# Where a relational GNN's second layer adds up its weight matrices: eight bases ahead of the first layer's edges, 22 as steps between its edge tiles

## The chip, the cores and the metric

The kernel runs on one core of a Trainium2 chip, in float32 but for a few small bfloat16 tables. The metric is the device time of one launch in microseconds (us). Three runs of the kernel before took 4658.36, 4662.56 and 4666.1 us; the median is 4662.56.

## The reference

Four parts follow one another: a relational graph network (RGCN) of two layers on 10000 nodes with 512 features, a mixture of experts, a second graph network (GINE) of four layers, and a feed-forward block with quantized weights. The change touches the first part alone, which is this, cut from the reference:

```python
def rgcn_gate_layer(x, row, col, edge_type, basis, att, gate_w, root, bias):
    w = jnp.einsum('rb,bio->rio', att, basis)      # 2 relations, 30 bases of 512x512
    x_j = x[col]                                   # 5000 edges
    msgs = []
    for r in range(NUM_RELATIONS):
        gate = jax.nn.sigmoid(x_j @ gate_w[r, :, 0])
        msgs.append(gate[:, None] * x_j @ w[r])
    msg = jnp.where((edge_type == 0)[:, None], msgs[0], msgs[1])
    agg = jax.ops.segment_sum(msg, row, num_segments=x.shape[0])
    return agg + x @ root + bias

h = jax.nn.relu(rgcn_gate_layer(x, row, col, edge_type, basis1, att1, gate_w1, root1, bias1))
out = rgcn_gate_layer(h, row, col, edge_type, basis2, att2, gate_w2, root2, bias2)
```

The first line of the layer is what the change moves: each relation's 512x512 weight matrix is a sum of 30 matrices ("bases"), each times a number. These sums depend on inputs alone, not on the nodes or edges.

## The kernel before

**Sorting.** `sort_edges` (L217) sorts the edges twice, by source (`by_src`, which the two RGCN layers use, 41 tiles of 128 edges, no tile with edges of both relations) and by target (`by_dst`, which the GINE part uses later). Tables of the sort are stored to memory and read again.

**Node pass.** `rgcn_nodes1` (L725) goes over the nodes in 20 blocks of 512: it loads `x_in`, normalizes it (`xn`, stored to `xn_d`), transposes it on PE and multiplies it by `root` (L742). ACT copies the product out of PSUM (L746), POOL adds the bias (L748), and SP stores the tile `o_nodes` to `r1_d` (the store's line is L139, in the helper `rows_to`). The edges' messages are later added into the same `r1_d`.

**Sums of bases.** `relation_weights` (L625) makes both weight matrices of a layer. For each of the 30 bases SP loads 1 MB into the tile `basis` (L630) out of the pool `stream`, which has two buffers (L755), and DVE adds it, times a number, into the two halves of `ws`, 128x2048 elements each (L635 for the first basis, L637 for the others). That is 60 sums on DVE for each layer.

**Placing.** `place_nodes` (L390) is a generator: it works out, for the GINE part, where the nodes' rows go, in 57 short steps of PE and DVE work. Its first step finds the ends of runs (`ends`), ten steps then compare four tiles of keys each (`equal_keys`, L212, output `eq`), six do tables of counts (`keyrep`, `base`, `row_ends`, `end`, `row_b`, `cum`), and the last 40 look up positions (L554, L567), the first of which also makes `wanted`.

**Edges.** `rgcn_edges` (L640) takes the 41 edge tiles through a pipeline written out by hand: in step i of its loop it

- fetches tile i: POOL gathers 128 rows of `xn_d` (layer 1) or `r1_d` (layer 2) into `x` (L614);
- adds up tile i - 5: PE multiplies `x` by the matrix `same` (L689), which sums rows of equal source, and ACT copies the result to `aT` (L693);
- puts tile i - 6: PE multiplies `aT` by the relation's weights (L703), ACT copies to `o` (L708), and POOL adds the rows into `r1_d` by an indirect DMA, the "scatter" (L619);
- makes tile i - 3 ready: DVE takes two products of `x` and the gate's vector (L669, output `prod`), ACT the sigmoid `g` (L674), DVE the choice by relation (L675, `dots`), PE spreads the keys (L680), and DVE makes `same` (L682);
- takes one step of `beside`, the generator that is handed in.

The loop stands under a manual schedule: PE, POOL, ACT and DVE each do its instructions in the order in which the code names them. Everything outside such a loop is put in order by the framework, which may move work of different parts between one another, and also into the loop's gaps. Each engine then works through its own list strictly in order, and so does SP, which issues the loads and stores of the node pass and of the bases: one that waits holds up all behind it.

Layer 1's loop takes a step of `place_nodes` at i = 6, 8, ..., 46 (21 steps), layer 2's at every i. Layer 2's `relation_weights` stands in the code between the two loops. Layer 2's first gather reads what the last scatter of layer 1 has written.

Of the kernel before, what the change touches and what calls it, by code (L numbers as in the profile page):

```python
# [8 lines left out]
F32 = mybir.dt.float32  # L9
# [4 lines left out]
OP = mybir.AluOpType  # L14
# [3 lines left out]
P = 128  # L18
N = 10000
D = 512  # L20
KC = D // P
# [17 lines left out]
RELATIONS = 2  # L39
# [3 lines left out]
CAP = 625  # L43
CT = (CAP + P - 1) // P
LAYERS = 4
FETCHED, READY = 6, 3
LN_EPS = 1e-5
BN_EPS = 1e-5
# [21 lines left out]
def gnn_ffn_kernel(ctx: ExitStack, tc: tile.TileContext, I, out, dram):  # L70
# [70 lines left out]
    def row_broadcast(pool, d, width, name):  # L141

        t = pool.tile([P, width], F32, name=name)
        nc.sync.dma_start(t, bass.AP(tensor=d.tensor, offset=d.offset, ap=[[0, P], [1, width]]))
        return t
# [477 lines left out]


    def relation_weights(basis, att_d, pool, stream, tag):  # L625
        att = row_broadcast(pool, att_d, RELATIONS * BASES, f"att_{tag}")
        ws = pool.tile([P, RELATIONS, KC * D], F32, name=f"w_{tag}")
        for b in range(BASES):
            t = stream.tile([P, KC, D], F32, name="basis")
            nc.sync.dma_start(t, basis[b].rearrange("(k p) o -> p k o", p=P))  # L630
            tf = t.rearrange("p k o -> p (k o)")
            for r in range(RELATIONS):
                c = att[:, r * BASES + b : r * BASES + b + 1]
                if b == 0:
                    nc.vector.tensor_scalar(ws[:, r], tf, c, None, op0=OP.mult)  # L635
                else:
                    nc.vector.scalar_tensor_tensor(ws[:, r], tf, c, ws[:, r], op0=OP.mult, op1=OP.add)  # L637
        return ws

    def rgcn_edges(tag, meta, src_d, relu, ws, gate_d, dst_d, beside, take):  # L640

        with ExitStack() as s:
# [67 lines left out]
            with tc.manual_schedule(engines={E_.PE, E_.Pool, E_.Activation, E_.DVE}):  # L712
                for i in range(RT + FETCHED):
                    if i < RT:
                        fetch(i)
                    if i >= FETCHED - 1 and i - FETCHED + 1 < RT:
                        add_up(i - FETCHED + 1)
                    if i >= FETCHED:
                        put(i - FETCHED)
                    if READY <= i < RT + READY:  # L720
                        make_ready(i - READY)
                    if take(i):
                        next(beside, None)

    def rgcn_nodes1(root, bias, pools):  # L725

# [25 lines left out]

    with ExitStack() as s:
        wpool = s.enter_context(tc.tile_pool(name="w_rel", bufs=1))
        stream = s.enter_context(tc.tile_pool(name="stream", bufs=2))  # L755
        src_meta = s.enter_context(tc.tile_pool(name="src_meta", bufs=1))
        wk = s.enter_context(tc.tile_pool(name="sort", bufs=1))
        place_wk = s.enter_context(tc.tile_pool(name="place_wk", bufs=1))
        ps = s.enter_context(tc.tile_pool(name="sort_ps", bufs=2, space=PSUM))
        with ExitStack() as n:  # L760
            ld = n.enter_context(tc.tile_pool(name="ld1", bufs=2))
            tp = n.enter_context(tc.tile_pool(name="tp1", bufs=2))
            fix = n.enter_context(tc.tile_pool(name="fix1", bufs=1))
            small = n.enter_context(tc.tile_pool(name="small1", bufs=3))
            pt = n.enter_context(tc.tile_pool(name="pt1", bufs=2, space=PSUM))
            po = n.enter_context(tc.tile_pool(name="po1", bufs=3, space=PSUM))
            zero = fix.tile([P, D], F32, name="zero")
            nc.gpsimd.memset(zero, 0.0)
            for d in (r1_d, a2_d, xf_d, x2_d):
                clear_spare(zero, d)  # L770
            root = load_square(fix, I["L0_gnn_root1"], "root")
            bias = row_broadcast(fix, I["L0_gnn_bias1"], D, "bias")
            by_src = sort_edges(
                "s", I["src"], I["dst"], I["edge_type_2"], by_src_d, wk, ps, src_meta, by_relation=True
            )
            by_src = add_targets(by_src, wk, ps, src_meta)
            by_dst = sort_edges(
                "d", I["dst"], I["src"], I["edge_weight1"].rearrange("e o -> (e o)"), by_dst_d, wk, ps,
                meta_pool,
            )  # L780
            rgcn_nodes1(root, bias, (ld, tp, small, pt, po))
            ws = relation_weights(I["L0_gnn_basis1"], I["L0_gnn_att1"], wpool, stream, "1")
        placing = place_nodes(by_dst, place_wk, ps, meta_pool)
        rgcn_edges(
            "1", by_src, xn_d, False, ws, I["L0_gnn_gate_w1"], r1_d, placing,
            lambda i: i >= FETCHED and i % 2 == 0,
        )
        ws = relation_weights(I["L0_gnn_basis2"], I["L0_gnn_att2"], wpool, stream, "2")
        rgcn_edges("2", by_src, r1_d, True, ws, I["L0_gnn_gate_w2"], a2_d, placing, lambda i: True)
        for _ in placing:  # L790
            pass

# [1028 lines left out]
```

## Time and profile before

| what | value |
| --- | --- |
| time, median of three runs | 4662.56 us |
| time of the profiled execution | 4666.98 us |
| its span, first to last instruction | 4665.2 us |
| mean granted clock of TensorE | 0.931 |
| busy: PE, DVE, ACT, POOL | 87%, 60%, 36%, 34% |
| basis sums after the first of each layer (L637) | 116, 315.8 us together |
| first gather of layer 1 | starts at 532.50 us |
| first gather of layer 2 | starts at 845.12 us |

Times in a profile count from the start of the span. The engines are PE (TensorE's matmuls; PEld is its weight loads), DVE (VectorE), ACT (ScalarE), POOL (GpSimd) and SP (SyncE, which here only issues transfers; its own queue is shown as SPq).

A table of windows has a row for each stretch of time: the busy time of each engine in it with the number of instructions, then the share of TensorE's full clock that was granted (PEclk), the busy share of the DMA engines, and GB/s. A row of a timeline has the start, the length, the engine, the line of the code, the operation, output<-input, and in brackets the idle time before it with what ended that idle time. On SPq the length of a group ("x3") is the time from its first issue to the end of its last. A row of the page's costliest groups has the count, the busy time together with the mean of one in nanoseconds, and the idle time before them with what ended most of it.

The releaser in brackets is inferred. Where the one named had long been done, the wait was for something else, often a transfer.

### The profile page before, as it was taken

The page shows a single profiled execution, that of the slowest core. Times are in us where ns is not written, and L with a number is a line of the kernel's source. Part 1 is how long each engine was busy: PE and PEld are TensorE (multiplying, and loading weights), DVE is VectorE, ACT ScalarE, POOL GpSimd, SP SyncE. Part 2 cuts the span into 40 slices and gives each one's busy share as a digit, 9 for nine tenths or more (in the row PEclk, how much of TensorE's full clock was granted, in tenths as well). Part 3 has the DMA queues.
Part 4 walks back from the last instruction along what each step waited for, and adds up shares of the span by engine and source line. Part 5 has one row for each costly group of instructions (what it writes and reads, how often), then busy time and mean ns, then how long its engine had stood idle before and what let it go on. Part 6 is the DMA issues. An engine that isn't in the chain of part 4 may idle for free.

```text
span 4665.2 us, 42798 instructions
## 1 busy us (share of the span) xinstructions
PE 4046.1 (87%) x13624; PEld 2048.0 (44%) x13624; DVE 2820.7 (60%) x5906; ACT 1679.5 (36%) x2992; POOL 1569.0 (34%) x1127
## 2 busy tenths in 40 slices
PE   6799568897999945968887999999999999999997
PEld 3443234443444422434443555545555455544443
DVE  7887865554545465646755546644575455755776
ACT  4334112232333310116423523354233532334775
POOL 3434334441000036865542113311142111422443
PEclk9899789898988866989889999999999999999998
DMA  8677654457555414986411123102231012311332
GB/s 276 228 260 258 216 123 88 86 105 184 192 171 182 146 48 84 162 164 218 153 54 43 73 77 119 42 17 81 85 108 37 27 75 104 90 30 46 110 109 98
DMA packets 293120, 556.20 MB, mean 119 GB/s; under 512 B 41216, under 2 KB 71969, under 8 KB 291871
## 3 DMA queue, kind: packets, MB, share of 16 engines
q1 hardware_dynamic: 219632, 364.67, 23.2%
q0 software_dynamic: 73264, 188.79, 17.8%
q8 instruction: 111, 1.82, 0.2%
q14 instruction: 113, 0.93, 0.1%
HBM read 292.40 MB, written 260.95 MB: 119 GB/s over the span
## 4 chain that ended last, share of the span: by engine, by line
PE 38%; DVE 8%; DMA 4%; ACT 3%; issue 2%; POOL 1%; POOLq 0%; DVEq 0%; ACTq 0%
PE ps_b L1317 15%; PE ps_d L1317 8%; PE ps_o L1593 5%; PE ps_e L1317 4%; PE ps_x L1424 2%; DMA x<-xg_d,gpos 2%; PE ps_x L1248 2%; ACT feat L1413 1%; DMA x_in<-x_d,node_at 1%; DVE stats L1402 1%; DVE x L1234 1%; DVE feat L1252 1%; PE ps_q L1661 1%; DVE feat L1332 1%; DVE t L1340 0%
## 5 line engine op out<-in xcount | busy, mean ns | idle before, releaser
L1317 PE MATMUL ps_b<-feat,w 128*128 128x512 f32 (+1 forms) x1120 | 499.7, 587 | 25.6 <-ACT feat L1413 25.5
L1317 PE MATMUL ps_d<-feat,w_s 128*128 128x512 f32 (+1 forms) x1120 | 503.6, 586 | 4.3 <-issue 3.1
L1325 ACT ACTIVATE feat<-ps_b,cols 128x512 f32<-128x512 f32 (+1 forms) x300 | 203.8, 683 | 568.1 <-PE ps_b L1317 555.4
L1352 POOL TENSOR_TENSOR feat<-feat 128x1024 f32<-128x1024 f32 (+1 forms) x70 | 162.5, 2322 | 623.2 <-DVE feat L1351 598.2
L1365 POOL TENSOR_TENSOR feat<-feat,p 128x1024 f32<-128x1024 f32 (+1 forms) x70 | 176.3, 2519 | 483.0 <-ACT feat L1325 474.2
L637 DVE SCALAR_TENSOR_TENSOR w<-basis,att,w 128x2048 f32<-128x2048 f32 x116 | 315.8, 2731 | 15.6 <-DMA basis<-in_L_gnn_basis 15.6
L742 PE MATMUL ps_o<-root,xT 128*128 128x512 f32 (+1 forms) x632 | 323.6, 625 | 0.0
L1317 PEld LDWEIGHTS ps_b<-feat,w 128*128 128x128 f32 x1120 | 208.4, 191 | 255.5 <-issue 209.4
L703 PE MATMUL ps_o<-w,aT 128*128 x656 | 304.6, 609 | 0.1
L1426 DVE TENSOR_TENSOR x_rows<-ps_x,be 128x512 f32<-128x512 f32 (+1 forms) x237 | 157.4, 685 | 231.0 <-PE ps_x L1424 231.0
L1317 PEld LDWEIGHTS ps_d<-feat,w_s 128*128 128x128 f32 x1120 | 203.3, 192 | 202.2 <-issue 183.0
L918 PE MATMUL ps_n<-root,rT 128*128 128x512 f32 (+1 forms) x632 | 288.6, 613 | 0.0
L1317 PE MATMUL ps_b<-t,w_s 128*128 128x512 f32 (+1 forms) x560 | 259.2, 603 | 21.7 <-ACT feat L1325 21.6
L1317 PE MATMUL ps_e<-feat,w 128*128 128x512 f32 (+1 forms) x560 | 264.9, 614 | 12.9 <-DVE feat L1283 12.9
L614 POOL DMA_INDIRECT x<-xg_d,gpos x160 | 175.0, 1093 | 287.8 <-issue 71.8
L1317 PE MATMUL ps_b<-feat,w_s 128*128 128x512 f32 (+1 forms) x560 | 253.7, 591 | 0.0
L1413 ACT ACTIVATE feat<-feat,bn_sm 128x512 f32<-128x512 f32 (+2 forms) x320 | 236.6, 809 | 3.4 <-DVE bn_sm L1532 3.4
L1234 DVE SCALAR_TENSOR_TENSOR x<-we,srt_d,x 128x512 f32<-128x512 f32 x160 | 139.9, 889 | 156.6 <-DMA x<-xg_d,gpos 149.5
L1402 DVE BATCH_NORM_STATS2 stats<-feat 128x6 f32<-128x512 f32 (+1 forms) x320 | 202.7, 667 | 46.7 <-POOL feat L1365 33.1
L1248 PE MATMUL ps_x<-same,x 128*128 128x128 f32 x1280 | 176.9, 287 | 58.6 <-DVE same L1244 24.1
L1248 PEld LDWEIGHTS ps_x<-same,x 128*128 128x128 f32 x1280 | 167.9, 199 | 126.9 <-issue 42.2
L1237 ACT ACTIVATE x<-x 128x512 f32<-128x512 f32 x160 | 99.3, 628 | 295.2 <-DVE x L1234 179.3
(483 smaller groups left out, 7656.1 us busy)
## 6 DMA issues: line engine op xcount, KB each, us to landing
basis<-in_L_gnn_basis SPq DMA_DIRECT2D x60, 1024.0 KB
xg_d<-x_rows SPq DMA_DIRECT2D x234, 256.0 KB
xg_d<-x_in SPq DMA_DIRECT2D x39, 512.0 KB
x_in<-in_x SPq DMA_DIRECT2D x19, 1024.0 KB
a_d<-x_in SPq DMA_DIRECT2D x19, 1024.0 KB
xn_d<-xn SPq DMA_DIRECT2D x19, 1024.0 KB
r_d<-o_nodes SPq DMA_DIRECT2D x19, 1024.0 KB
r_in<-r_d SPq DMA_DIRECT2D x19, 1024.0 KB
```

What stands on the lines that cost most here:

```text
L637: nc.vector.scalar_tensor_tensor(ws[:, r], tf, c, ws[:, r], op0=OP.mult, op1=OP.add)
L703: nc.tensor.matmul(ps_o, lhsT=aT[:, k, :], rhs=w_all[:, bass.ds(w0 + k * D, D)], start=k == 0, stop=k == KC - 1,)
L742: nc.tensor.matmul(ps_o[:n], lhsT=xT[:, k, a * P : a * P + n], rhs=root[:, k, :], start=k == 0, stop=k == KC - 1,)
L918: nc.tensor.matmul(ps_o[:n_], lhsT=rT[:, k, a * P : a * P + n_], rhs=root[:, k, :], start=k == 0, stop=k == KC - 1,)
L1234: nc.vector.scalar_tensor_tensor(x, we, by_dst["attr"][:, t : t + 1], x, op0=OP.mult, op1=OP.add)
L1248: nc.tensor.matmul(ps_a[:, k, :], lhsT=x[:, k * P : (k + 1) * P], rhs=same, start=True, stop=True)
L1317: nc.tensor.matmul(ps[fo], lhsT=A[a][:, k, fo * P : (fo + 1) * P], rhs=x[:, k, :], start=first and k == 0, stop=k == 1, skip_group_check=True,
L1325: nc.scalar.activation(dst[:, fo, :], ps[fo], func, bias=b, scale=scale)
L1365: nc.gpsimd.tensor_tensor(b22, b22, p5, OP.add)
L1402: nc.vector.bn_stats(stats[:, k, 2 * p + j, :], big[:, k, s0 + j * w : s0 + (j + 1) * w])
L1413: nc.scalar.activation(hb, hb, AF.Relu, bias=sm[:, fo, 3:4], scale=sm[:, fo, 2:3])
L1593: nc.tensor.matmul(ps_o[:n_], lhsT=big[:, kc, t * P : t * P + n_], rhs=W2[kc], start=kc == 0, stop=kc == KC - 1,)
```

## The change

`relation_weights` now returns the weights' tile and a generator that adds one basis (two sums) at each step. All 30 bases of layer 1 are still added before its edges. Of layer 2's bases, eight (`EARLY_BASES`) are added before layer 1's edges, and the other 22 inside layer 1's edge loop, one at each even i from 4 to 46, behind the work that makes a tile ready. The steps of `place_nodes` move to the odd i from 7 to 45, which is 20 instead of 21; the one left over falls to layer 2's loop, which as before takes one at every i. The pool `stream` has three buffers instead of two.

```diff
--- before.py
+++ after.py
@@ -43,6 +43,7 @@
 CAP = 625
 CT = (CAP + P - 1) // P
 LAYERS = 4
+EARLY_BASES = 8
 FETCHED, READY = 6, 3
 LN_EPS = 1e-5
 BN_EPS = 1e-5
@@ -623,21 +624,26 @@
 
 
     def relation_weights(basis, att_d, pool, stream, tag):
+
         att = row_broadcast(pool, att_d, RELATIONS * BASES, f"att_{tag}")
         ws = pool.tile([P, RELATIONS, KC * D], F32, name=f"w_{tag}")
-        for b in range(BASES):
-            t = stream.tile([P, KC, D], F32, name="basis")
-            nc.sync.dma_start(t, basis[b].rearrange("(k p) o -> p k o", p=P))
-            tf = t.rearrange("p k o -> p (k o)")
-            for r in range(RELATIONS):
-                c = att[:, r * BASES + b : r * BASES + b + 1]
-                if b == 0:
-                    nc.vector.tensor_scalar(ws[:, r], tf, c, None, op0=OP.mult)
-                else:
-                    nc.vector.scalar_tensor_tensor(ws[:, r], tf, c, ws[:, r], op0=OP.mult, op1=OP.add)
-        return ws
-
-    def rgcn_edges(tag, meta, src_d, relu, ws, gate_d, dst_d, beside, take):
+
+        def sums():
+            for b in range(BASES):
+                t = stream.tile([P, KC, D], F32, name="basis")
+                nc.sync.dma_start(t, basis[b].rearrange("(k p) o -> p k o", p=P))
+                tf = t.rearrange("p k o -> p (k o)")
+                for r in range(RELATIONS):
+                    c = att[:, r * BASES + b : r * BASES + b + 1]
+                    if b == 0:
+                        nc.vector.tensor_scalar(ws[:, r], tf, c, None, op0=OP.mult)
+                    else:
+                        nc.vector.scalar_tensor_tensor(ws[:, r], tf, c, ws[:, r], op0=OP.mult, op1=OP.add)
+                yield
+
+        return ws, sums()
+
+    def rgcn_edges(tag, meta, src_d, relu, ws, gate_d, dst_d, beside):
 
 
 
@@ -719,8 +725,7 @@
                         put(i - FETCHED)
                     if READY <= i < RT + READY:
                         make_ready(i - READY)
-                    if take(i):
-                        next(beside, None)
+                    beside(i)
 
     def rgcn_nodes1(root, bias, pools):
 
@@ -752,7 +757,7 @@
 
     with ExitStack() as s:
         wpool = s.enter_context(tc.tile_pool(name="w_rel", bufs=1))
-        stream = s.enter_context(tc.tile_pool(name="stream", bufs=2))
+        stream = s.enter_context(tc.tile_pool(name="stream", bufs=3))
         src_meta = s.enter_context(tc.tile_pool(name="src_meta", bufs=1))
         wk = s.enter_context(tc.tile_pool(name="sort", bufs=1))
         place_wk = s.enter_context(tc.tile_pool(name="place_wk", bufs=1))
@@ -779,14 +784,26 @@
                 meta_pool,
             )
             rgcn_nodes1(root, bias, (ld, tp, small, pt, po))
-            ws = relation_weights(I["L0_gnn_basis1"], I["L0_gnn_att1"], wpool, stream, "1")
+            ws1, adding = relation_weights(I["L0_gnn_basis1"], I["L0_gnn_att1"], wpool, stream, "1")
+            for _ in adding:
+                pass
+            ws2, adding = relation_weights(I["L0_gnn_basis2"], I["L0_gnn_att2"], wpool, stream, "2")
+            for _ in range(EARLY_BASES):
+                next(adding)
         placing = place_nodes(by_dst, place_wk, ps, meta_pool)
+
+        def beside_1(i):
+            if i >= 4 and i % 2 == 0:
+                next(adding, None)
+            elif i > FETCHED:
+                next(placing, None)
+
+        rgcn_edges("1", by_src, xn_d, False, ws1, I["L0_gnn_gate_w1"], r1_d, beside_1)
+        for _ in adding:
+            pass
         rgcn_edges(
-            "1", by_src, xn_d, False, ws, I["L0_gnn_gate_w1"], r1_d, placing,
-            lambda i: i >= FETCHED and i % 2 == 0,
+            "2", by_src, r1_d, True, ws2, I["L0_gnn_gate_w2"], a2_d, lambda i: next(placing, None)
         )
-        ws = relation_weights(I["L0_gnn_basis2"], I["L0_gnn_att2"], wpool, stream, "2")
-        rgcn_edges("2", by_src, r1_d, True, ws, I["L0_gnn_gate_w2"], a2_d, placing, lambda i: True)
         for _ in placing:
             pass
```

## The prediction

> **What bounds the stretch now.** The page says that TensorE is busy for 87% of the span, but the change touches only the stretch between the end of the node pass and layer 2's edges. So I read that stretch first by windows, then each queue's timeline.
>
> ```profile
> core 0: us, PE busy (x) PEld busy (x) DVE busy (x) ACT busy (x) POOL busy (x), PEclk, DMA share, GB/s
> 440.00:510.00 70.00, 69.07 (x205) 31.80 (x204) 54.03 (x38) 23.49 (x45) 29.49 (x9) 1.00 0.69 220
> 510.00:541.00 31.00, 0.18 (x1) 0.00 (x0) 20.88 (x11) 0.53 (x1) 11.82 (x8) 0.57 0.78 259
> 541.00:626.00 85.00, 33.84 (x105) 18.92 (x105) 80.00 (x98) 8.49 (x19) 21.23 (x11) 0.68 0.69 199
> 626.00:845.00 219.00, 180.47 (x676) 98.34 (x675) 104.97 (x397) 45.16 (x105) 93.10 (x68) 0.95 0.48 84
> ```
>
> Four stages with four limits. Until 510 the node pass fills PE, and sums of bases on DVE lie beside it for nothing. Until 541 PE is empty. Until 626 DVE is full (80.00 of 85) and PE waits. From 626 neither PE nor DVE is full, though DVE has 114 us idle. I look for the cause of the empty 31 us in the timelines of SP and POOL.
>
> ```profile
> 504.88 12.51 SPq L630 DMA_DIRECT2D basis<-in_L_gnn_basis  x3
> 517.49 0.46 SPq L139 DMA_DIRECT2D r_d<-o_nodes  x1
> ...
> 522.18 1.21 SPq L139 DMA_DIRECT2D r_d<-o_nodes  x2
> ```
>
> ```profile
> 507.14 7.70 POOL L748 TENSOR_TENSOR o_nodes<-o_nodes,bias 128x1024 f32<-128x1024 f32 x2 [4.43 <-ACT o_nodes L746]
> 532.50 3.14 POOL L614 DMA_INDIRECT x<-xn_d,gidx_s  x1 [17.66 <-DVE w L637]
> ...
> 572.38 3.51 POOL L619 DMA_INDIRECT r_d<-o,sidx  x1 [2.32 <-DVE dots L675]
> ...
> 649.32 1.59 POOL L619 DMA_INDIRECT r_d<-o,sidx  x1 [2.55 <-ACT g L674]
> ...
> 834.20 1.55 POOL L619 DMA_INDIRECT r_d<-o,sidx  x1 [3.93 <-issue]
> 839.71 1.55 POOL L619 DMA_INDIRECT r_d<-o,sidx  x1 [3.95 <-DMA r_d<-o,sidx]
> 845.12 1.01 POOL L614 DMA_INDIRECT x<-r_d,gidx_s  x1 [3.86 <-DMA r_d<-o,sidx]
> ```
>
> The last bias add ends at 514.84, but its r1_d store stands on SP behind basis loads that wait for DVE to free one of two buffers, and goes out only at 522.18. The first gather of layer 1 shares memory with these tiles, starts at 532.50, and the first product with the gate starts at 540.99. Scatters of layer 1 form a chain: each waits for the one before to land, 839.71 − 834.20 = 5.5 us apart. Last, DVE in the steady part, first and last line one pair of tiles apart:
>
> ```profile
> 642.83 0.34 DVE L212 SCALAR_TENSOR_TENSOR eq<-ps_s,key_d,below 128x128 f32<-128x128 f32 x1
> ...
> 649.18 0.16 DVE L675 SCALAR_TENSOR_TENSOR dots<-g,of_rel 128x2 f32<-128x2 f32 x1 [3.25 <-ACT g L674]
> ...
> 653.62 0.16 DVE L675 SCALAR_TENSOR_TENSOR dots<-g,of_rel 128x2 f32<-128x2 f32 x1 [2.41 <-ACT g L674]
> ...
> 654.22 0.34 DVE L212 SCALAR_TENSOR_TENSOR eq<-ps_s,key_d,below 128x128 f32<-128x128 f32 x1
> ```
>
> A pair takes 11.39 us, against 11.0 for two scatters: the chain of scatters is nearly the bound, and DVE waits twice for the sigmoid g, which stands on ACT behind the copy of ps_o.
>
> ```profile
> L637 DVE SCALAR_TENSOR_TENSOR w<-basis,att,w 128x2048 f32<-128x2048 f32 x116 | 315.8, 2731 | 15.6 <-DMA basis<-in_L_gnn_basis 15.6
> ```
>
> **The change, part by part.** No instruction is added or removed. What moves, by the written order of both kernels: before, the framework put 24 of layer 2's 60 sums into layer 1's first ten tiles, one behind each DVE instruction, 20 into the second half of the node pass and the rest earlier. After, 16 sums stand before the edges and 44 in the loop, two back to back at even steps. A sum alone is 2.3 us (2.35 in rows of this stretch; the group's mean of 2731 ns takes in ones slowed by transfers).
>
> *Start of the edges.* No basis load waits in front of the last r1_d stores any more, for three are fetched ahead into the three buffers and the next ones come inside the loop. The FFN's small loads now stand before those stores on SP; what they wait for was done by about 490, so I cost them at nothing, and 4 to 7 us if that cover fails. The stores go out at 515 to 516 instead of 522.18. A scatter lands 3.95 us after its issue; before, from the end of the last store's issue to the gather took 532.50 − 523.39 = 9.1 us with basis transfers in flight. I take the near one: gather at 520, bounds 519 to 525. From gather to product took 8.5 us here and 4.25 us at layer 2's start (845.12 to 849.37), where no basis was in flight; as here none will be, I take 4.25. First product at 524.5 instead of 541.0: **16.5 us** earlier (bounds 7 to 19).
>
> *First tiles.* Tiles 0 to 6 take about 2.35 us of DVE each (two products 1.43, sigmoid 0.3, same 0.6): 16.5; three pairs of sums 13.8; place_nodes' step of ends 3.3 (ten small DVE instructions of place_nodes took 733.94 to 736.1, 2.2 us, and this one has two more copies that wait for PE): 33.6 us, where before the same tiles took some 90.
>
> *Ten pairs with a step of equal_keys.* Call its first eq Z. Dots follow at Z + 6.35, as above (649.18 − 642.83). PE's part is unchanged, as PE is released by the second eq. Then same is done at Z + 6.95, two sums to Z + 11.55, the next tile's products 1.43 to 12.98, its sigmoid and same at once, for PE and ACT ran ahead during the sums: next Z at 13.88. So 4.6 us of sums cost **2.5 us**, and the rest goes into the second wait for g. Ten pairs: 138.8 us. The scatters' 11.0 is no longer the bound.
>
> *Seven pairs with place_nodes' later steps* took 733.94 to 815.12 before, 81.2 us; with 2.3 us each 97.3. The last three scatters 16.6 (at 5.5). Sum of the loop 33.6 + 138.8 + 97.3 + 16.6 = 286 against 845.1 − 541.0 = 304.1: 18 us less.
>
> *The clock.* PE would idle about 4.1 us in each of the 17 pairs, while DVE sums. The granted clock fell to half after an idle PE in three places of this stretch, 3.6 to 4.8 us after its last work:
>
> ```profile
> 514.00:515.00 1.00, 0.00 (x0) 0.00 (x0) 1.00 (x1) 0.00 (x0) 0.84 (x1) 0.65 0.02 8
> 515.00:516.00 1.00, 0.00 (x0) 0.00 (x0) 1.00 (x1) 0.00 (x0) 0.00 (x0) 0.50 0.00 0
> ```
>
> PE's last work here ended at 510.18. After a restart at 630.55 it was back at 633.8, so 3.2 us at half speed, a loss of 1.6 us. Bounds per pair 0 and 1.6; 4.1 lies amid 3.6 to 4.8, so I take 0.7, or **12 us** for 17 pairs.
>
> [...]
>
> *Rest.* Two more sums now stand before the last store of the sort: 4.7 us of DVE, of which I count 2, as PE's backlog of transposes and matmuls (69.07 of 70 busy) covers much of it. One place_nodes step moves from layer 1 to layer 2, at most 0.8 us (the median step there has three DVE instructions of 0.48, most of it in DVE's idle time). Layer 2 and the later three stages stay as they are; what is free there starts earlier by the gain.
>
> *The sum.* 16.5 + 18 − 12 − 2 = **20 us**. The profiled execution of before took 4666.98 us (span 4665.2); after: 4647. It lies 4.4 above the median of the three runs, 4662.56, so the median goes to **4643**.
>
> **The rivals.**
>
> *The clock halves in every gap.* 27 instead of 12: gain 5, median 4657, no change that can be told. For it: 4.1 us is longer than the shortest of the three observations. Against it: two of three were longer.
>
> *The chain of scatters stays the bound, and gets slower.* In the early edges of before, with sums and basis transfers beside them, scatters took up to 3.51 us to issue instead of 1.59, and the way from gather to product 8.5 us instead of 4.25. Now each pair has two sums and a load of 1 MB beside it. If each scatter gets 0.5 us longer in issue and 2.1 us in landing, a pair takes 2 × 8.2 = 16.4 us instead of 14.6 (13.88 + 0.7): 17 × 1.9 = 32 us lost, 12 us slower than before, median 4675. This decides from 15.8 us per pair, where 17 × 1.2 eats the 20. For it: chain and DVE are within 3 us of each other. Against it: the window from 510 to 541 moved 259 GB/s, by which a load of 1 MB lasts some 4 us of 14, so it meets one scatter in two at most.
>
> [...]
>
> *More is gained.* The clock holds in every gap: gain 32, median 4631; with a node pass freed of DVE's sums and loads, down to 4620.
>
> *It does not do what it says.* The framework interleaved the sums before as well; if the start at 541 is set by something else than the stores (the trace names a DVE sum as releaser of the first gather), the 16.5 us shrink to 7 and the gain to 10: 4653, about the edge of what can be told.
>
> **How the numbers follow.** Forecast 0.47 (its own range 4627 to 4653), clock at each gap 0.13, slower chain 0.22, more gained 0.10, start that does not move 0.08. The range leaves out the ends of the slow and the large case: 4615 to 4682. A measurement of this kernel tells about 0.2%, 9.3 us, from no change. Faster by over 0.2%: nearly all of the forecast and of the large case, and half of the last, 0.59; within: the clock's case, the rest of the last and edges, 0.19; slower 0.22.
>
> **What would show it.** Right: first gather near 520, r1_d stores on SP without a basis load between them; scatters 14 to 15 us per pair; sums in twos on DVE; the second wait of dots for g gone; layer 2's first gather near 825 and its 232 us unchanged. Wrong: scatters 16 us per pair with each waiting for DMA r_d (slower chain), or a clock below 0.8 in the loop, or a first gather still behind 530.

## The result, and the profile after

The changed kernel took 4664.49 us (median of 12 runs, 4656.93 to 4673.24), the kernel before 4656.73 us in the same job (12 runs, 4646.18 to 4666.10). The ratio is 1.0017, with a 95% interval of 1.0007 to 1.0027: 7.8 us slower, within the 0.2% that I called no change, and on the other side of the forecast 20 us gain. The size rests on this one set of runs: in the four later ones the kernel before had medians of 4662.03 to 4664.37 us, about the time of the changed kernel here. What is sure is that the gain did not come.

The two profiled executions alone would mislead: 4666.98 us before, 4658.06 after, 9 us the other way. In the 17 profiles of this study, what comes behind layer 2's last gather, which no kernel here changes, takes from 3594.8 to 3608.2 us (3608.0 in before's, 3594.8 in after's). So I compare profiles only up to that gather: 1057.17 us before, 1061.54 after, 4.4 us later, of the timing's sign. A second profile of the changed kernel puts it at 1061.41.

Windows of the changed kernel, the same stretches as for before:

```profile
core 0: us, PE busy (x) PEld busy (x) DVE busy (x) ACT busy (x) POOL busy (x), PEclk, DMA share, GB/s
440.00:510.00 70.00, 69.13 (x197) 30.97 (x197) 33.45 (x48) 25.06 (x48) 25.07 (x11) 0.95 0.76 220
510.00:541.00 31.00, 19.39 (x60) 10.01 (x60) 10.73 (x19) 5.87 (x12) 15.04 (x10) 0.78 0.48 159
541.00:626.00 85.00, 64.10 (x213) 35.77 (x211) 57.29 (x140) 15.54 (x36) 35.88 (x22) 0.86 0.57 142
626.00:845.00 219.00, 163.65 (x533) 90.92 (x533) 150.44 (x343) 37.19 (x84) 87.74 (x53) 0.84 0.53 128
```

Of the empty 31 us behind 510, 19.39 are filled with PE work, DVE is no longer full behind 541, and from 626 DVE has 45 us more to do, as intended. But PEclk fell from 0.95 to 0.84 in the long last stretch. The timelines of SP and POOL show the start of the edges:

```profile
512.82 0.35 SPq L145 DMA_DIRECT2D gate<-in_L_gnn_gate_w  x1
515.07 9.74 SPq L140 DMA_DIRECT2D r_d<-o_nodes  x3
541.07 84.73 SPq L634 DMA_DIRECT2D basis<-in_L_gnn_basis  x7
```

```profile
523.22 1.25 POOL L753 TENSOR_TENSOR o_nodes<-o_nodes,bias 16x512 f32<-16x512 f32 x1 [1.13 <-ACT o_nodes L751]
526.93 1.01 POOL L615 DMA_INDIRECT x<-xn_d,gidx_s  x1 [2.46 <-DMA r_d<-o_nodes]
...
604.23 1.59 POOL L620 DMA_INDIRECT r_d<-o,sidx  x1 [6.75 <-ACT g L680]
...
609.62 1.74 POOL L620 DMA_INDIRECT r_d<-o,sidx  x1 [1.73 <-DVE w L641]
...
620.34 1.59 POOL L620 DMA_INDIRECT r_d<-o,sidx  x1 [7.70 <-ACT g L680]
...
852.25 1.01 POOL L615 DMA_INDIRECT x<-r_d,gidx_s  x1 [4.09 <-DMA r_d<-o,sidx]
```

No basis load stands among the r1_d stores, and the first gather follows the last bias add by 2.46 us. But that bias add ends at 524.47 instead of 514.84: the node pass got 9.6 us longer. In the loop a pair takes 620.34 − 604.23 = 16.1 us. POOL waits 6.7 to 8.3 us (4.9 in the first of these pairs), for ACT, ahead of each first scatter of a pair, so the chain of scatters is not the bound. DVE shows one whole pair and more:

```profile
604.09 0.16 DVE L681 SCALAR_TENSOR_TENSOR dots<-g,of_rel 128x2 f32<-128x2 f32 x1 [4.59 <-ACT g L680]
...
604.69 4.60 DVE L641 SCALAR_TENSOR_TENSOR w<-basis,att,w 128x2048 f32<-128x2048 f32 x2
...
610.97 0.16 DVE L681 SCALAR_TENSOR_TENSOR dots<-g,of_rel 128x2 f32<-128x2 f32 x1 [0.33 <-ACT g L680]
...
611.57 0.34 DVE L213 SCALAR_TENSOR_TENSOR eq<-ps_s,key_d,below 128x128 f32<-128x128 f32 x1
...
620.20 0.16 DVE L681 SCALAR_TENSOR_TENSOR dots<-g,of_rel 128x2 f32<-128x2 f32 x1 [5.53 <-ACT g L680]
...
627.69 0.34 DVE L213 SCALAR_TENSOR_TENSOR eq<-ps_s,key_d,below 128x128 f32<-128x128 f32 x1
```

From dots at 604.09 to Z at 611.57 it takes 7.48 us, against 13.88 − 6.35 = 7.53 in the forecast, and the second wait for g is gone. But from Z to the dots it takes 8.63 us instead of 6.35. That part is PE's, and PE and its clock say why (the second fence is a table of windows, same columns as above):

```profile
607.67 0.38 PE L212 MATMUL ps_s<-ident,key_d 128*128 128x128 f32 x2
611.98 0.95 PE L212 MATMUL ps_s<-ident,key_d 128*128 128x128 f32 x2 [3.92 <-DVE eq L213]
612.72 1.92 PE L695 MATMUL ps_a<-same,x 128*128 128x128 f32 x8
```

```profile
606.95:610.36 3.41, 1.10 (x5) 0.38 (x3) 3.38 (x5) 0.58 (x1) 1.68 (x2) 1.00 0.62 138
610.36:613.77 3.41, 1.79 (x7) 1.50 (x8) 2.65 (x14) 0.20 (x1) 1.98 (x2) 0.50 0.86 287
613.77:617.18 3.41, 3.41 (x9) 1.86 (x8) 0.86 (x4) 0.58 (x1) 0.00 (x0) 0.50 0.72 176
617.18:620.60 3.42, 3.42 (x16) 2.00 (x15) 0.29 (x3) 0.80 (x3) 0.26 (x1) 1.00 0.01 2
```

PE ends at 608.05 and waits 3.92 us. The clock is at half from 610.36, before the wait is over, and comes back only at 617.18, 5.2 us after PE has restarted; eight ps_a matmuls take 1.92 us in place of 1.07 (at full clock, at 643.87 in before). The ten pairs with equal_keys run from Z = 563.43 to 723.29, 15.99 us each, and the clock falls once for each, about where it starts. In seven of them it is at half for 6.83 us, and these pairs take 16.1 to 16.7 us; in three for 3.41 us, and these take 15.1 to 15.2.

### The profile page after: what moved, and what is told of

Same layout as the page of the kernel before. It is cut to its first block, busy times and chain, and to the rows that moved or that the text cites. A ratio compares the mean times of both kernels' runs of the same rounds, so it can differ in the third digit from the quotient of the medians.

```text
span 4656.3 us, 42795 instructions
## 1 busy us (share of the span) xinstructions
PE 4061.7 (87%) x13624; PEld 2058.8 (44%) x13624; DVE 2814.8 (60%) x5906; ACT 1681.5 (36%) x2992; POOL 1570.6 (34%) x1127
## 4 chain that ended last, share of the span: by engine, by line
PE 38%; DVE 8%; DMA 4%; ACT 3%; issue 2%; POOL 1%; DVEq 0%; POOLq 0%; ACTq 0%
PE ps_b L1334 14%; PE ps_d L1334 9%; PE ps_o L1610 5%; PE ps_e L1334 4%; PE ps_x L1441 2%; DMA x<-xg_d,gpos 2%; PE ps_x L1265 2%; DVE stats L1419 1%; ACT feat L1430 1%; DVE feat L1269 1%; DMA x_in<-x_d,node_at 1%; DVE x L1251 1%; PE ps_q L1678 1%; DVE feat L1349 1%; DVE t L1357 1%
## 5 line engine op out<-in xcount | busy, mean ns | idle before, releaser
L709 PE MATMUL ps_o<-w,aT 128*128 x656 | 315.2, 626 | 0.0
L641 DVE SCALAR_TENSOR_TENSOR w<-basis,att,w 128x2048 f32<-128x2048 f32 x116 | 301.9, 2619 | 0.0
L1334 PE MATMUL ps_b<-t,w_s 128*128 128x512 f32 (+1 forms) x560 | 250.2, 586 | 17.7 <-ACT feat L1342 17.7
L1368 DVE TENSOR_TENSOR feat<-feat,t 128x1024 f32<-128x1024 f32 (+1 forms) x70 | 83.9, 1198 | 199.4 <-PE ps_b L1334 199.4
```

The costliest lines, as they stand in the source:

```text
L709: nc.tensor.matmul(ps_o, lhsT=aT[:, k, :], rhs=w_all[:, bass.ds(w0 + k * D, D)], start=k == 0, stop=k == KC - 1,)
L1334: nc.tensor.matmul(ps[fo], lhsT=A[a][:, k, fo * P : (fo + 1) * P], rhs=x[:, k, :], start=first and k == 0, stop=k == 1, skip_group_check=True,
```

## The experiments

Theory 1: the granted clock falls in every pair while DVE sums, and that is the loop's loss. Theory 2, the rival of the prediction: the chain of scatters, slowed by sums and loads, sets the pair. The start was open, so one run repeats the kernel.

**after_again**: the changed kernel unchanged.

> The changed kernel once more, for a second profile. In the first one the node pass ended 9.6 us later than before (last bias add ended at 524.47 instead of 514.84) and the key column of the second sort was copied at 483.52 instead of 469.67. If that comes from the order of the sums, it is there again within 3 us. If it is an accident of one execution (the phase of the clock's windows, or transfers), the two times move by more than 3 us. Pairs of edge tiles 15.9 us again by either.

The key column of the second sort was copied at 483.51, the last bias add began at 523.16 and layer 2's first gather at 852.21: each within 0.1 us of the first profile. So the 9.6 us are not an accident of one execution. (The clock's windows are the steps of 3.41 us in which its records change, shown under why the prediction was wrong.) The time was 4664.99 us.

**warm**: extra matmuls at the end of even steps.

```diff
+            def keep_warm():
+                ps_k = pk.tile([P, P], F32, name="ps_k")
+                for _ in range(8):
+                    nc.tensor.matmul(ps_k, lhsT=ident, rhs=ident, start=True, stop=True)
...
                     beside(i)
+                    if not relu and i >= 4 and i % 2 == 0 and i < RT + READY:
+                        keep_warm()
```

> The changed kernel with eight extra matmuls of 128x128 into ps_k at the end of every even step of layer 1's edges, whose result nobody reads; they lie in the 3.9 us in which PE waits for DVE's sums. Theory 1 (the clock): in every pair of tiles PE idles 3.9 us, the granted clock falls to half and costs 2.1 us of a pair's 15.95. With PE busy the clock stays at 1.00, a pair takes 13.9 us, and from the first gather of layer 1 to that of layer 2 it takes 325 - 17 x 2.1 = 290 us; the kernel gets 30 to 35 us faster than the changed one, so about 25 faster than before. Theory 2 (the chain of scatters, slowed by sums and loads, sets 15.95): extra PE work changes nothing or costs up to 1 us per pair, 4664 to 4680.

The kernel took 4674.9 us, ratio 1.0029 (1.0015 to 1.0044): slower. The clock did hold: 1.00 from 545 to 720, and a pair took 14.86 us, 1.1 less than before the extra matmuls, not 2.1. They wait for `same` (PE idle for 1.43 us ahead of them), and so push back the next tile's matmuls, whose result DVE then waited for (1.37 us instead of 0.33). Later steps lost more than the first pairs gained. It told against theory 2, but priced the clock badly.

**warm_late**: the same kind of matmuls behind the odd tile's work, in a place where nothing waits for them.

```diff
             elif i > FETCHED:
+                spare = ps.tile([P, 2 * LO], F32, name="ps_r", bufs=1)
+                for _ in range(10 if i < RT + READY else 0):
+                    nc.tensor.matmul(spare[:, :P], lhsT=ident, rhs=ident, start=True, stop=True)
                 next(placing, None)
```

> The changed kernel with ten extra matmuls of 128x128 in every odd step of layer 1's edges, behind the tile's own work on PE and ahead of place_nodes' step, into a PSUM tile that nothing else uses then (ps_r); nobody reads them. In the run warm the clock held at 1.00, but the extra matmuls stood ahead of the next tile's work, and a pair took 14.9. Here they lie behind it, in the last 3 us of PE's wait. Theory 1 (the clock's fall makes a pair 15.95 instead of 13.88): a pair takes 13.9 us, from first gather to first gather 285 to 300 instead of 325, the kernel 4630 to 4645. If instead the extra time of a pair came from elsewhere and warm's 14.9 was a bound of PE's own work, a pair stays at 14.9 or above and the kernel at 4650 or above.

4644.79 us, ratio 0.9963 (0.9950 to 0.9976). PE and DVE in one pair:

```profile
611.99 2.40 PE L801 MATMUL ps_r<-ident 128*128 128x128 f32 x20
614.23 0.38 PE L212 MATMUL ps_s<-ident,key_d 128*128 128x128 f32 x2
616.31 0.32 PE L212 MATMUL ps_s<-ident,key_d 128*128 128x128 f32 x1 [1.70 <-DVE eq L213]
```

```profile
602.06 0.34 DVE L213 SCALAR_TENSOR_TENSOR eq<-ps_s,key_d,below 128x128 f32<-128x128 f32 x1
...
608.41 0.16 DVE L681 SCALAR_TENSOR_TENSOR dots<-g,of_rel 128x2 f32<-128x2 f32 x1 [3.25 <-ACT g L680]
...
615.90 0.34 DVE L213 SCALAR_TENSOR_TENSOR eq<-ps_s,key_d,below 128x128 f32<-128x128 f32 x1
```

Z to Z is 13.84 us, the forecast's 13.88 without the clock, and dots follow Z by 6.35 again. Work that computes nothing made the kernel 0.5% faster than the changed one, so theory 1 stands for these ten pairs: they took 140.1 us instead of 159.9. In one of them the clock fell all the same, for 3.41 us from 673.44, and this pair (from Z = 671.25 to 686.78) took 15.53 us. The seven pairs with other steps did not gain (105.8 us against 106.1, with a clock of 0.88 from 700 to 835); their excess over the forecast 97.3 is not settled by this. From first gather to first gather it took 310.8, more than expected for that reason.

**in_waits**: one sum in each tile's wait for g, instead of two behind every second tile.

```diff
                 nc.scalar.activation(g[:, :RELATIONS], dots, AF.Sigmoid)
+                inside(t)
...
-            if i >= 4 and i % 2 == 0:
-                next(adding, None)
-            elif i > FETCHED:
+            if i > FETCHED and i % 2 == 1:
                 next(placing, None)
+        def inside_1(t):
+            for _ in range(2 if t < 3 else 1):
+                next(adding, None)
```

> The changed kernel with its 44 sums inside the loop moved: one sum in each tile, between DVE's products and dots, where DVE waits for the sigmoid g (2.4 and 3.2 us in the pairs of the kernel before), two in each of the first three tiles. Theory 1: sums of 2.3 us lie in waits, PE is never idle for more than about 2 us, the clock stays at 1.00, and a pair takes 11.0 (two scatters of 5.5) to 12.5 us; from first gather to first gather 255 to 275 us instead of 325, the kernel 4595 to 4615. Theory 2: sums and loads beside the scatters slow these wherever the sums stand: a pair stays at 14 us or more, 4640 or above.

4637.45 us, ratio 0.9947 (0.9934 to 0.9961): the same 44 sums, at another place in the same list, and 0.7% faster than the changed kernel. DVE between two Z:

```profile
607.31 0.34 DVE L213 SCALAR_TENSOR_TENSOR eq<-ps_s,key_d,below 128x128 f32<-128x128 f32 x1
...
610.33 2.35 DVE L641 SCALAR_TENSOR_TENSOR w<-basis,att,w 128x2048 f32<-128x2048 f32 x1
613.66 0.16 DVE L682 SCALAR_TENSOR_TENSOR dots<-g,of_rel 128x2 f32<-128x2 f32 x1 [0.98 <-ACT g L680]
...
618.70 0.34 DVE L213 SCALAR_TENSOR_TENSOR eq<-ps_s,key_d,below 128x128 f32<-128x128 f32 x1
```

11.39 us, exactly the pair of the kernel before, which has no sums there. But only the three pairs from 595.92 to 630.09 are like this; the other six between the first and the last Z took 13.1 to 13.7. The clock did not stay at 1.00 as expected: it was 0.91 from 545 to 720, and fell at the start of four of the six. And scatters came 12.9 us per pair in this stretch and fell behind, until the loop stopped for them (16.0 us in the pair that ends with the scatter at 637.3). It took 299.7 us from first gather to first gather, not 255 to 275, and the kernel missed the 4595 to 4615 expected. Here theory 2 is half right.

**in_waits_no_loads**: in_waits without the 1 MB loads inside the loop.

```diff
-                t = stream.tile([P, KC, D], F32, name="basis")
-                nc.sync.dma_start(t, basis[b].rearrange("(k p) o -> p k o", p=P))
+                if tag == "1" or b <= EARLY_BASES:
+                    t = stream.tile([P, KC, D], F32, name="basis")
+                    nc.sync.dma_start(t, basis[b].rearrange("(k p) o -> p k o", p=P))
```

> As in_waits, but the 21 last bases of layer 2 are not loaded: their sums take the ninth base again, so the values differ and the 1 MB loads inside the loop are gone. It prices the loads. In in_waits scatters came 12.9 us per pair in the stretch from 560 to 630, where DVE's own pair was 11.4. If the loads in flight slow the scatters' landing, scatters come 11.4 to 11.6 per pair and layer 2's first gather comes 15 to 30 us earlier than 828. If DVE's sums themselves slow them (their issue on POOL), it stays at 12.5 or more.

This kernel leaves out 21 loads and so computes other values. One run of 4609.54 us; layer 2's first gather at 796.20 instead of 828.01, 3 us of it by an earlier first gather of layer 1 (525.26). Scatters on POOL:

```profile
603.20 1.59 POOL L620 DMA_INDIRECT r_d<-o,sidx  x1 [2.73 <-DVE eq L213]
...
608.98 1.59 POOL L620 DMA_INDIRECT r_d<-o,sidx  x1 [2.54 <-ACT g L681]
...
614.51 1.59 POOL L620 DMA_INDIRECT r_d<-o,sidx  x1 [2.65 <-DVE eq L213]
```

11.3 us per pair beside the same sums, from 595 to 630 at a clock of 1.00 as in in_waits: it is the loads in flight that slow the scatters there, by 1.6 us per pair or more, for without them DVE's own pair of 11.39 may set the pace. The sums alone do not make 12.9.

**The number of early bases**, in four kernels. Only the constant (or, in the in_waits kernels, also who gets the remaining sums) differs.

```diff
-EARLY_BASES = 8
+EARLY_BASES = 5      # early_5: 3 bases left for behind the loop
+EARLY_BASES = 18     # early_18: 12 bases left as steps
```

> The changed kernel with 5 instead of 8 of layer 2's bases ahead of layer 1's edges, as many as the kernel before had ahead of the second sort's end; 22 stay as steps and 3 come after layer 1's loop. If sums ahead of the sort's end delayed it, the key column of the second sort is copied 5 us or more earlier than 483.5 and the node pass ends at 520 or before. If the delay is the clock's or an accident, it is as in the changed kernel. The last three bases cost up to 14 us between the layers.

> The changed kernel with 18 instead of 8 of layer 2's bases ahead of layer 1's edges; by the written order the ten more stand behind the second sort's end, where DVE is idle from 483 to 526, and 12 bases are left as steps. Theory 1: the ten fill DVE's idle time while PE ends the node pass; r1_d stores stand behind basis loads again, the first gather comes at 531 to 537 instead of 527; ten pairs lose their sums and go from 15.95 to 11.4 us, so layer 2's first gather comes near 852 + 7 - 45 = 814, the kernel 4620 to 4635. If the node pass itself gets slower by the loads (transfers that its own loads and stores wait for), it ends after 535 and half of the gain is lost.

> As in_waits (one sum in each tile's wait for g), with 5 instead of 8 bases ahead of the edges; the last three bases are added in the first three steps of layer 2's loop, where DVE waits for the last scatters. Theory: sums ahead of the second sort's end delay it. As in early_5, the sort's key column comes 10 us and the first gather 5 us earlier than in in_waits (528.3), and nothing else changes: layer 2's first gather near 823, the kernel 4628 to 4636. If the six sums moved to layer 2 are not hidden, they cost up to 14 us there.

> Both ways together: 18 bases ahead of the edges, and the other 24 sums one by one in the waits for g of every second tile (each of the first eight). In in_waits DVE's own pair was 11.4 us where the clock held, but scatters beside sums and loads came 12.9 us per pair. With half as many sums and loads per pair the scatters come 11.4 to 12 us per pair: from first gather to first gather 265 to 275 instead of 300, the first gather at 531 to 537, the kernel 4612 to 4622. If the chain of scatters is slow for another reason, it stays at 12.9 and the kernel is not below 4635.

early_5 (one run, 4675.2 us): the sort's key column came at 473.69, the first gather at 521.95, 5 us earlier; the three bases behind the loop took it back (layer 2's first gather at 861.33). in_waits_5 (one run, 4648.07): key column 478.80, first gather 527.18, 1.1 us earlier; layer 2's first gather 835.94, 8 us later, and I don't know what took these. early_18, 4667.34 us, ratio 1.0011 (1.0001 to 1.0021): forecast 4620 to 4635, a clear miss. SP and POOL:

```profile
533.82 1.46 SPq L140 DMA_DIRECT2D r_d<-o_nodes  x1
537.88 4.89 SPq L634 DMA_DIRECT2D basis<-in_L_gnn_basis  x2
```

```profile
545.74 1.01 POOL L615 DMA_INDIRECT x<-xn_d,gidx_s  x1 [23.61 <-DMA r_d<-o_nodes]
```

The last r1_d store stood behind basis loads until 533.82 and landed beside two more about 10.5 us after its issue had ended (535.28 to 545.74); the first gather came 18.8 us later than in the changed kernel, and the ten pairs without sums (11.2 to 14 us) gave back only 22. DVE summed without a break until 542, so the idle time it was to fill was shorter than the ten bases. in_waits_18, 4646.95 us, ratio 0.9959 (0.9945 to 0.9973), has the same late start (first gather 555.42) and a loop of 278 us; it missed the 4612 to 4622 expected, too.

**in_waits_11**: 11 bases early, and 38 sums, one in each tile from the fourth.

> As in_waits, with 11 instead of 8 of layer 2's bases ahead of the edges and the other 38 sums one by one in the waits for g of tiles 3 to 40. In early_18 DVE worked on sums until 542 and the stores of r1_d landed beside basis loads 12 us after their issue, so the first gather came at 546. Theory: three more bases end at about 500, well before the node pass (524), so the first gather stays at 525 to 532, the first three tiles lose three sums (7 us), and layer 2's first gather comes near 820 instead of 828; the kernel 4625 to 4635. If any base more ahead of the edges costs what it saves, it is 4637 to 4645.

4639.0 us, ratio 0.9953 (0.9936 to 0.9969). First gather 531.34, layer 2's 817.58, as expected; the time was not below in_waits.

**The third buffer**, taken from the changed kernel and given to the kernel before.

```diff
-        stream = s.enter_context(tc.tile_pool(name="stream", bufs=3))
+        stream = s.enter_context(tc.tile_pool(name="stream", bufs=2))   # bufs_2, bufs_2_timed; before_bufs_3 the other way
```

> The changed kernel with two buffers of bases instead of three, nothing else. The third buffer lets a load go out one base earlier. If it matters to the start, the first gather comes later than 527 by up to one sum pair (5 us) or the second sort's end moves by more than 3 us from 483.5; the pairs of edge tiles stay at 15.9, as their loads have 16 us of time with either.

> The kernel before with three buffers of bases instead of two, nothing else. If the third buffer delays the second sort's end (469.7 before, 483.5 after) by its loads, the key column is copied at 475 or later here; if the order of the sums does, it stays within 3 us of 469.7. The loop's start stays behind basis loads, first gather 530 or later, and the kernel within 10 us of before.

> The changed kernel with two buffers again (as bufs_2), now timed against before. In bufs_2 the second sort ended at 458.4 instead of 483.5 and the first gather came at 503.1 instead of 526.9; layer 2's first gather at 829.4 instead of 852.2. If that is the order that the framework writes for two buffers, it is there again within 1 us, and the kernel takes 4664 - 23 = 4641 (4636 to 4648), 0.3 to 0.6% faster than before. If it was an accident of one execution, the second sort ends near 483 again and the kernel takes 4655 or more.

The copy of the key column on DVE's timeline (L368 and L367 are the same copy), first in the changed kernel:

```profile
483.52 0.19 DVE L368 COPY key_d<-srt_d 128x40 f32<-128x40 f32 x1 [11.33 <-DMA srt_d<-by_dst_d]
```

In bufs_2:

```profile
458.36 0.82 DVE L368 COPY key_d<-srt_d 128x40 f32<-128x40 f32 x1 [11.58 <-DMA srt_d<-by_dst_d]
```

In bufs_2_timed, the same kernel:

```profile
463.10 0.76 DVE L368 COPY key_d<-srt_d 128x40 f32<-128x40 f32 x1 [11.58 <-DMA srt_d<-by_dst_d]
```

In the kernel before:

```profile
469.67 0.86 DVE L367 COPY key_d<-srt_d 128x40 f32<-128x40 f32 x1 [11.51 <-DMA srt_d<-by_dst_d]
```

In before_bufs_3:

```profile
482.99 0.20 DVE L367 COPY key_d<-srt_d 128x40 f32<-128x40 f32 x1 [11.38 <-DMA srt_d<-by_dst_d]
```

Three buffers end the sort 20 to 25 us later in the changed kernel, 13 us later in the kernel before. The other profiles with eight early bases agree: the copy stands at 480.63 to 484.93 in six with three buffers, and at 457.10 to 463.10 in three with two. The first gather of the changed kernel moves from 526.93 to 503.06 and 507.75. The 4.7 us between two executions of one kernel were not expected. The loop did not change (322.8 and 321.9 us from first product to layer 2's first gather, 321.8 with three). bufs_2 took 4645.75 us in one run; timed, 4654.43, ratio 0.9990 (0.9974 to 1.0006), half of the expected gain over the changed kernel. before_bufs_3 took 4654.48 in one run: its later start (first gather 549.89) is given back by a loop that begins with fewer sums.

What the buffer does is in the order that the framework writes. With three, 73 sums instead of 70 stand on DVE ahead of the key column's copy, in both kernels, and SP has one or two basis loads more ahead of most of the node pass's later loads (of the 15th, 16th and 17th piece of x_in: 22, 25 and 27 instead of 21, 23 and 26). early_5 and in_waits_5 have 70 sums there with three buffers, and copy at 473.69 and 478.80. The ten profiles with three buffers and 73 sums range from 478.42 (early_18) to 487.89 (in_waits_18), so only the first of the two lies outside them, and what the count does is not settled. From 300 to 440 the clock is 0.96 to 1.00 with two buffers in before, bufs_2 and bufs_2_timed, and 0.92 to 0.93 with three in the changed kernel and before_bufs_3; but in_waits_11_bufs_2, with two, has 0.94 like in_waits_11 with three. From bufs_2 (1.00) to bufs_2_timed (0.96) that is 0.04 × 140 = 5.6 us of full clock, which would fit the 4.7 us; from bufs_2 to the changed kernel (0.93) it is about 10 of the 25 us (estimates from these rows). Whether the order costs its time through this clock was not tried.

**Both causes away**: in_waits and in_waits_11 with two buffers.

> in_waits with two buffers: both causes taken away at once, the sums in DVE's waits for g and the node pass in the order of two buffers. If the two add up, the first gather comes at 503 to 506, layer 2's at 828 - 24 = 804, and the kernel takes 4638 - 23 = 4615 (4608 to 4624). If loads with two buffers come too late for one sum in each tile, DVE waits for basis loads and scatters come 14 us per pair or more: 4630 or above.

> in_waits_11 with two buffers. In in_waits_11 the first gather came 10.7 us after the last bias add's end, beside basis loads, and layer 2's first gather at 817.6. With two buffers the node pass ends 20 to 24 us earlier: layer 2's first gather at 795 to 800 if the three more bases still end before the node pass does, 805 if they do not (they have 24 us less); the kernel 4608 to 4622.

in_waits_bufs_2: first gather 501.92, layer 2's 806.04 (804 expected), 4631.84 us, ratio 0.9948 (0.9931 to 0.9965). in_waits_11_bufs_2: first gather 520.49, layer 2's 814.17, 4630.75 us, ratio 0.9936 (0.9913 to 0.9960). In the first the profile adds up. In the second it does not: layer 2's first gather was expected at 795 to 805 and came 3.4 us earlier than in in_waits_11, its sort having ended at 466.15, and its first gather again 11 us behind the last bias add, as in in_waits_11. Both missed the times expected (4608 to 4624 and 4608 to 4622). The timed gain is the same as in_waits' within the intervals: both beat the kernel before by some 0.5 to 0.6%, and which is best can't be told.

## Why the prediction was wrong

In profiled time, up to layer 2's last gather, the forecast had 1037 (1057.17 − 20); it was 1061.54. By its own steps:

- **Start of the edges.** From the end of the last bias add to the first product: 26.15 us before, 9.7 forecast, 5.98 measured. This mechanism was right, its gain undersized; gather to product took 3.5 us, not 4.25.
- **Rest.** "4.7 us of DVE, of which I count 2" was the failed step here. The node pass ended 9.6 us later and the sort 13.9. It wasn't the eight early bases: the buffer alone, at the same number of bases, moves the sort's end by 20 to 25. I had costed the third buffer as three loads ahead and did not follow what it does to the order of the node pass. One count was off without weight: before, DVE does 30 of layer 2's sums behind the first product, not 24. All in all the first product came 10.5 us earlier, not 14.5.
- **First tiles.** 33.0 us measured, 33.6 forecast.
- **Ten pairs.** 159.9 us instead of 138.8. DVE's two parts, 6.35 and 7.53, were right within 0.1 us, as warm_late's 13.84 shows; the clock cost 2.1 us per pair. The 2.3 us of a sum held, too (4.60 for two). The longer ones in before's mean of 2731 ns are not shown to come from transfers: 13 of the 116 took 3.34 to 6.92 us, each beside one of POOL's bias adds (L748), and 136 GB/s moved during them on average, against 245 during the 102 of 2.31 to 2.35 us.
- **The clock** was the step that failed. I took 0.7 us per pair with an upper bound of 1.6, from one restart of 3.2 us at half speed and from three falls 3.6 to 4.8 us after PE's last work; in the ten pairs it cost 2.1. Two of the three, at 514.30 and 585.98, came 4.1 and 4.8 us after PE's last matmul; the 3.6 fits the fall at 626.94 counted from the last ps_o (623.38), but PE ended two ps_s at 626.05, 0.9 us before it. In the changed kernel the fall came 2.3 to 3.8 us after PE's last matmul (4.9 in the first pair), and the half speed lasted 3.41 or 6.83 us, up to 6.3 of it after the restart. So the bound was wrong as well as the value: a single restart is no upper bound where its length varies. The trace of before held more than the three falls: seven between 510 and 845 us, and ahead of five of them PE had been at work for 0.54 to 1.12 of the last 3.41 us, as in this fall at 746.41:

```profile
743.00:746.41 3.41, 0.88 (x8) 0.86 (x9) 2.90 (x12) 0.00 (x0) 0.78 (x2) 1.00 0.66 140
746.41:749.82 3.41, 3.41 (x8) 1.86 (x8) 1.85 (x6) 0.59 (x1) 3.00 (x3) 0.50 0.47 49
```

- **Seven late pairs and the tail.** 106.1 and 22.9 us instead of 97.3 and 16.6. warm_late shortened neither (105.8 and 28.5), so this is not settled. In the tail, scatters came 6 to 7 us apart instead of 5.5, though the last basis load had gone out at 810.25, before the tail began (829.35); what slowed them stays open.
- **Layer 2.** 209.3 us from its first to its last gather, 212.05 before.

Together: 10.5 earlier, 17.7 longer in the loop (321.8 against 304.1), 2.8 shorter in layer 2, so 4.4 later, 24 us off the forecast. Of these, 14 are the clock in the ten pairs (159.9 against 138.8 and 7 for the clock), 4 the start (the node pass took 7.6 more than the 2 counted, the way to the first product gave 3.7 back), 4 the late pairs and 6 the tail; first tiles and layer 2 give 3 back. So the largest part is shown to be the clock, the buffer's part is shown but not its mechanism, and the 10 us of late pairs and tail are open. The likeliest case was wrong; the rival of a clock that halves in every gap had the right mechanism for the ten pairs, was given 0.13, and was priced at 27 us for 17 pairs, 1.6 each. The rival of the slower scatter chain fell for the changed kernel: POOL waited for ACT, not for the scatter before. It holds where the pair is short enough, as in in_waits.

The clock's records explain the size. In every trace here the clock changes only on a grid of 3.41 us, whose phase differs from trace to trace (from the fall at 610.36 in the changed kernel to that at 746.41 in before it is 39.9 steps); the rows of the round from 606.95 to 620.60 above stand on it. Between 530 and 860 us of the 17 traces, each of the 158 windows of this grid that were at full clock and had PE busy for less than 1.4 us ended with a fall, and of the 961 with 1.75 us or more all but one did not; between the two it went either way. In before and after alone these are 22 of 22 and none of 106. In the one from 606.95 to 610.36 PE worked for 1.10 us, and the clock fell at its end. The clock came back at the end of a window that PE had filled (3.09 us or more in 188 of 189). So PE's wait in these pairs (3.9 us, 6.1 in the first) brought one window at half speed in three of them and two in seven, as it lay on the grid, and the pairs repeat by threes: from Z = 563.43 to 611.57, 659.40 and 707.21 it takes 48.1, 47.8 and 47.8 us, and 14 windows of 3.413 are 47.8.

## What to carry to other kernels

Work that is moved into a loop on one engine is priced by where it stands in that engine's list: two sums behind the work of every second tile stalled PE for 3.9 us and cost 4.6 us per pair, 2.1 of it through the clock, while the same sums, one by one in waits that DVE had anyway, cost DVE's pair nothing where the clock held and the scatters kept up (11.39 us in in_waits, as in before). When a change lets PE idle in every round, read all the falls of the clock that the trace has (here each window of 3.41 us at full clock in which PE worked for less than 1.4 us ended in one), and take the length from several restarts and not from one (3.41 or 6.83 us in the ten pairs). A buffer more was not free here, where the framework decides the order (the second sort ended 13 to 25 us later): compare the written order of all stages that share a queue with it, not just the one it is meant for.

## What was not expected of the hardware

The granted clock fell 2.3 us after PE's last matmul (608.05 to 610.36), and half speed lasted up to 6.83 us, though PE was full from its restart on. The first gather came 2.1 us after the last r1_d store's issue where no load was in flight (524.81 to 526.93, 15 GB/s moved), and 10.5 us after it beside 1 MB loads (early_18). Scatters slowed from 5.65 to 6.45 us apart on average beside such loads (in_waits_no_loads and in_waits), at an unchanged 1.59 us of issue in most rows. And two executions of one kernel put the same instruction of the node pass 4.7 us apart, while two of another kernel agreed within 0.1 us.
